# Second attention of a four-layer kernel: another buffer for beta, the first gate behind both beta halves, and another order of the statistics, the decay scan and k's turn

## The chip, the cores and the metric

The kernel runs on one core of a Trainium2 chip. A core has five engines with a queue of instructions each: TensorE (PE in the profile; PEld is its weight load, which overlaps the matmuls), VectorE (DVE), ScalarE (ACT), GpSimd (POOL) and SyncE (SP, which here only issues transfers). An engine works through its own queue in order; between engines, semaphores hold an instruction back until what it needs is there. Besides these there are 16 DMA engines.

The metric is the device time of one execution, in microseconds. The kernel before took 1192.94 us, the median of three runs.

## The reference

The model has four residual layers on x (1024 tokens of 256 channels): softmax attention, a layer of 8 experts, the second attention, and a layer of 16 experts with 4 chosen for each token. Layer norms stand in front of and behind each. The change is in the second attention alone. Its reference, cut:

```python
q, k, v = hidden_states @ Wq, hidden_states @ Wk, hidden_states @ Wv
beta = jax.nn.sigmoid(hidden_states @ Wb + bb)
gate = silu(hidden_states @ Wg)
q = silu(causal_dwconv(q, qconv_w, qconv_b))     # 4 taps along the tokens, channel by channel
k = silu(causal_dwconv(k, kconv_w, kconv_b))
q = layernorm(q.reshape(Bs, Ls, H, DK), qn_w, qn_b)   # H = 16 heads, DK = DV = 128
k = layernorm(k.reshape(Bs, Ls, H, DK), kn_w, kn_b)
...
def step(S, inp):
    q_t, k_t, v_t, b_t = inp
    S = (1.0 - b) * S + b * (v_t[..., :, None] * k_t[..., None, :])
    o_t = jnp.einsum('bhvk,bhk->bhv', S, q_t)
    return (S, o_t)
_, os = lax.scan(step, S0, (qs, ks_, vs, bs))
return (o * gate) @ Wo
```

beta is one number for each token and head. The state S of a head, a 128 x 128 matrix, decays by 1 - beta with each token and takes in v times k.

## The kernel before

All matrices are float32. The normed input lies in SBUF as hT, channels on partitions, 1024 tokens along the row. The recurrence is not run token by token: the tokens are cut into 8 chunks of 128, inside a chunk the output comes from a masked product of q and k, and between chunks the state is carried on.

`attention1` (from L1032) has these parts.

- **beta and decay, once for all heads.** `shares` makes beta for one half of the tokens: two matmuls into pb (L1066) and a Sigmoid on ACT (L1069). `decays` turns beta to tokens on partitions for the values (L1079), forms decay = 1 - beta and scans it to running products prod (L1083). With the second half done, both go to DRAM as `rows` (L1089, L1090), since each head needs its own row of them spread over all partitions. beta, decay, begin and prod borrow buffers from the two-buffer pool `two` by giving the tag of a tile that is used later; beta has the tag "y".
- **`convolved`, for k and for q of each head.** Two px instructions of PE for each half of the tokens (L1115) into a PSUM tile px, of which there are two; four taps into y (the first on ACT, L1101, the other three on DVE, L1107; in head 0 for each half by itself, otherwise for all 1024 tokens at once); a Silu on ACT (L1125). Next come eight transposes of y on PE (L1134), BN statistics on DVE (L1136), and a chain of small operations: difference d of the two half means (L1143), mean (L1144), d squared (L1145, in place), variance ve (L1146 to L1149), its power -1/2 on POOL (L1150), shift (L1151). Then ACT scales the eight blocks to sn (L1155), PE transposes them back (L1163), and ACT writes kn or qn (L1164). It is a generator with a yield between these steps: the first half's px; the second half's px with taps and Silu; transposes and statistics; sn; the turn back.
- **`values`**, for two heads at once: four pv tiles (L1185), each multiplied by beta on DVE (L1190).
- **`enter(h)`** prepares a head: it calls the generators k_, q_ and v_ in a written order, computes the output gate (`gated`: two matmuls pg, L1219, for each half of the tokens, and a Silu, L1223), has the head's rows of decay and products spread by two transfers (L1238), and scans the spread decay to dec (L1253), the decay between any two tokens of a chunk. In head 0 it also calls `shares` and `decays`, and `catch_up`, which issues the turning of hT's last tiles (L281) that the layer before has left over.
- **`attend(h)`** uses the head: qg on POOL (L1280); for each half of the chunks pk (transposes of kn, L1291), ke (L1293), the scores psc (L1301), pr (L1303), pkv (L1308) and the states (L1316, L1319); then for each half po (L1327, L1331) and og, the output times the gate (L1335). After each odd head follows the output projection of two heads, 32 matmuls (L846), added up in L858 (the first one copied, L856).

**What sets the order.** `attend(h)` is a generator too, and `enter(h + 1)` is advanced by one step at each of its yields:

```python
for _ in enter(0):
    pass
for h in range(H):
    ahead = enter(h + 1) if h + 1 < H else iter(())
    for _ in attend(h):
        next(ahead, None)
    for _ in ahead:
        pass
```

So a head's preparation lies between the pieces of the head before. The framework then reorders the instructions of each engine by its own plan, except those that are `pinned` (L210, kept in program order); what results is a fixed queue for each engine. pk, psc, pkv, po, pg, pv, pb and all transposes share one PSUM pool of four tiles (tag "b1"), so that a tile's next user waits for the reader of the one four tiles ago.

A pair of heads is: the even head (its odd partner is prepared in it), then the odd head with the output projection at its end (the next pair's even head is prepared in it).

Of the kernel before, what the change touches and what calls it, by code (L numbers as in the profile page):

```python
# [10 lines left out]
AF = mybir.ActivationFunctionType  # L11
ALU = mybir.AluOpType
# [15 lines left out]
DK = 128  # L28
# [35 lines left out]
class Net:  # L64
# [967 lines left out]
    def attention1(self):  # L1032
        nc, tc, a = self.nc, self.tc, self.a
        C = P
        NC = T // C
        with ExitStack() as ctx:
# [5 lines left out]
            idr = one.tile([P, NC, C], F32, name="idr")  # L1042
# [9 lines left out]
            two = ctx.enter_context(tc.tile_pool(name="c_two", reuse_waits="tile", bufs=2))  # L1052
            beta, decay, begin, prod = (
                two.tile([H, NC, C], F32, tag=t, name=s)
                for t, s in (("y", "beta"), ("qg", "decay"), ("sn", "begin"), ("gate", "prod"))
            )

            def flat(v):
# [36 lines left out]
            def convolved(h, hh, w, cw, cb, nw, nb, z):  # L1095

                px = ps2.tile([P, T], F32, tag="x2", name="px")
                y = two.tile([P, T], F32, tag="y", name="y")
# [13 lines left out]
                for hf in range(2):  # L1112
                    c = slice(hf * HALF, (hf + 1) * HALF)
# [25 lines left out]
                def new(name):  # L1139
                    return self.small.tile([P, NC], F32, tag=name, name=name)  # L1140

                d, mean, ve, rs, shift = (new(s) for s in ("d8", "mean8", "ve8", "rs8", "shift8"))
                nc.vector.tensor_tensor(d, st[:, :, 1], st[:, :, 4], ALU.subtract)  # L1143
                nc.vector.scalar_tensor_tensor(mean, d, -0.5, st[:, :, 1], ALU.mult, ALU.add)  # L1144
                nc.vector.scalar_tensor_tensor(d, d, 0.25, d, ALU.mult, ALU.mult)  # L1145
                nc.vector.scalar_tensor_tensor(  # L1146
                    ve, st[:, :, 2], DK * EPS, st[:, :, 5], ALU.add, ALU.add
                )
                nc.vector.scalar_tensor_tensor(ve, ve, 1.0 / DK, d, ALU.mult, ALU.add)  # L1149
                nc.gpsimd.tensor_tensor(rs, ve, self.nhalf, ALU.pow)  # L1150
                nc.vector.scalar_tensor_tensor(shift, mean, -1.0, rs, ALU.mult, ALU.mult)  # L1151
                yield
                sn = two.tile([P, NC, P], F32, tag="sn", name="sn")
# [45 lines left out]
            def enter(h):  # L1199

                g, hh = divmod(h, HG)
                if hh == 0:
                    begin_group(g)
                wq, wk, wv, wg, wo, og, vb = groups[g]
                kn = two.tile([P, T], F32, tag="kn", name="kn")
                qn = two.tile([P, T], F32, tag="qn", name="qn")
                dec = two.tile([P, NC, C], F32, tag="dec", name="dec")
                spread = two.tile([P, 2, T], F32, tag="spread", name="spread")
                gate = two.tile([P, T], F32, tag="gate", name="gate")
                heads[h] = (kn, qn, dec, spread[:, 1, :], gate)  # L1210
                k_ = convolved(h, hh, wk, C_KCW, C_KCB, C_KNW, C_KNB, kn)
                q_ = convolved(h, hh, wq, C_QCW, C_QCB, C_QNW, C_QNB, qn)
                v_ = values(g) if hh == 0 else iter(())

                def gated(hf):
                    c = slice(hf * HALF, (hf + 1) * HALF)
                    pg = ps.tile([P, HALF], F32, tag="b1", name="pg")
                    for k in range(KC):
                        nc.tensor.matmul(  # L1219
                            pg, wg[:, k, hh * DK : (hh + 1) * DK], self.hT[:, k, c],  # L1220
                            start=(k == 0), stop=(k == KC - 1),
                        )
                    nc.scalar.activation(gate[:, c], pg, AF.Silu)  # L1223

                next(k_)
                if h == 0:

                    shares(0)
                    next(q_)
                    decays(0)  # L1230
                    next(v_)
                    next(v_)
                    gated(0)
                    self.catch_up(ps, len(self.todo))
                    shares(1)
                    decays(1)
                for i in range(2):
                    nc.sync.dma_start(out=spread[:, i, :], in_=rows[i, h, :].partition_broadcast(P))  # L1238
                next(k_)
                yield  # L1240
                if h > 0:
                    next(v_, None)
                    next(v_, None)
                yield
                if h > 0:
                    next(q_)
                next(q_)
                next(k_)
                yield
                next(v_, None)  # L1250
                next(v_, None)

                nc.vector.tensor_tensor_scan(  # L1253
                    dec.rearrange("p c t -> p (c t)"), spread[:, 0, :],
                    idr.rearrange("p c t -> p (c t)"), 0.0, ALU.mult, ALU.add,
                )
                yield
                next(k_)
                next(q_)
                yield  # L1260
                for hf in range(2):
                    if (h, hf) != (0, 0):
                        gated(hf)
                yield
                next(k_)
                next(q_)
                yield
                next(q_)
                yield
# [740 lines left out]
```

## Time and profile before

| | |
|---|---|
| three runs | 1192.67, 1192.94, 1194.61 us |
| profiled execution | 1203.99 us |
| its span in the profile | 1202.3 us |
| mean granted TensorE clock | 0.983 |
| instructions | 15820 |
| second attention | about 480 to 996 us |
| PE, DVE, ACT, POOL busy in these 516 us | 482.0, 364.6, 238.1, 94.7 us |

All times that follow come from the profiled execution, which took 11 us more than the median of the runs. "First scores of head h" is the start of that head's first psc matmul; the distance between two heads' first scores is the time that one head takes:

| head | first scores, us |
|---|---|
| 0 | 533.61 |
| 1 | 562.43 |
| 2 | 597.14 |
| 4 | 658.23 |
| 6 | 718.80 |
| 7 | 743.93 |
| 8 | 779.75 |
| 14 | 962.92 |
| 15 | 983.68 |

How to read the lines that follow: a row of the timeline has start, duration, engine, line, operation, tile written and tile read with partitions x elements, and a count if several were joined (x4 px matmuls and so on). A row of the waits has the engine, what stood waiting, the engine and instruction it waited for, then the sum in us, the number of times and the longest. A row of the windows has the stretch, its length and the busy time of each engine with the number of instructions.

### The profile page before, as it was taken

Reading aid. Unit: us, or ns where it says so; the run is one execution under the profiler, and the core shown is the slowest. Engines: PE = TensorE matmul, PEld = TensorE weight load, DVE = VectorE, ACT = ScalarE, POOL = GpSimd, SP = SyncE. Lnnn points to the kernel's source line nnn. Section 1 sums busy time; section 2 is a strip of 40 time slices with the busy share of each in tenths; the row PEclk is TensorE's granted clock in tenths of the full one; section 3 lists DMA queues with packets and bytes.
Section 4 is the critical chain, followed back from the end, with each engine's and each line's share of the span. In section 5 each row is a group of like instructions: output and inputs, shape, how many; then the busy total and the mean of one; then the engine's idle time right before and its main releaser. Section 6 shows DMA issues by size and latency. Waiting matters only on the chain. (4 is left out here: it accounts for less than half of the span.)

```text
span 1202.3 us, 15820 instructions
## 1 busy us (share of the span) xinstructions
PE 1124.2 (94%) x6002; PEld 688.6 (57%) x6002; DVE 707.3 (59%) x1682; ACT 519.5 (43%) x975; POOL 222.6 (19%) x209
## 2 busy tenths in 40 slices
PE   6999999998999999789999999999999987789996
PEld 3543333332457566356767676766676776447775
DVE  5876767761534335577677777777676857233224
ACT  4266666667131111445444454544444444223331
POOL 3100000000100000111111112121212124444662
PEclk9999999999999999999999999999999998899999
DMA  6000000000005101211313131222212114154844
GB/s 207 1 1 1 1 2 1 1 1 1 1 1 194 53 1 44 68 51 36 114 43 92 65 93 64 85 72 63 77 53 86 37 64 178 55 171 123 203 45 115
DMA packets 53495, 77.01 MB, mean 64 GB/s; under 512 B 7209, under 2 KB 44408, under 8 KB 53414
## 3 DMA queue, kind: packets, MB, share of 16 engines
q1 hardware_dynamic: 46886, 69.02, 18.0%
q0 software_dynamic: 6528, 6.93, 3.1%
q8 instruction: 49, 0.80, 0.3%
q14 instruction: 32, 0.26, 0.1%
HBM read 60.93 MB, written 17.00 MB: 65 GB/s over the span
## 5 line engine op out<-in xcount | busy, mean ns | idle before, releaser
L506 DVE TENSOR_REDUCE pm<-sc 128x1 f32<-128x512 f32 x256 | 163.2, 685 | 64.5 <-PE sc L570 43.2
L570 PE MATMUL sc<-qTm,kT 32*128 32x512 f32 x512 | 151.5, 644 | 1.9 <-ACT pe L588 1.9
L599 ACT ACTIVATE pe<-sc 128x512 f32<-128x512 f32 x216 | 117.8, 595 | 67.8 <-PE sc L570 47.3
L1155 ACT ACTIVATE sn<-pt,shift,rs 128x128 f32<-128x128 f32 x256 | 93.7, 470 | 106.9 <-DVE shift L1151 106.9
L501 PE MATMUL sc<-kT,qT 32*128 32x512 f32 x512 | 136.2, 637 | 1.6 <-ACT qT L460 0.8
L1115 PE MATMUL px<-hT,w_l1a 128*128 128x512 f32 x256 | 125.0, 600 | 5.4 <-DVE y L1107 5.1
L1107 DVE SCALAR_TENSOR_TENSOR y<-px,cp,y 128x1023 f32<-128x1023 f32 (+5 forms) x102 | 123.4, 1213 | 3.9 <-ACT y L1101 3.8
L1150 POOL TENSOR_TENSOR rs<-ve,nhalf 128x8 f32<-128x8 f32 x32 | 52.4, 1637 | 304.7 <-DVE ve L1149 249.9
L831 DVE TENSOR_TENSOR mid<-sg,pu 128x512 f32<-128x512 f32 (+1 forms) x50 | 32.0, 642 | 117.3 <-PE pu L828 100.8
L830 ACT ACTIVATE sg<-pg 128x512 f32<-128x512 f32 (+1 forms) x50 | 27.7, 562 | 134.2 <-PE pg L828 116.9
L232 POOL TENSOR_TENSOR rss<-ve,nhalf 128x2 f32<-128x2 f32 x12 | 8.4, 699 | 406.2 <-DVE ve L231 401.4
L557 PE MATMUL po<-pe,va 128*32 128x256 f32 (+1 forms) x872 | 79.6, 432 | 1.3 <-ACT oT L562 0.8
L570 PEld LDWEIGHTS sc<-qTm,kT 32*128 32x128 f32 x512 | 49.6, 184 | 54.3 <-issue 38.6
L1219 PE MATMUL pg<-hT,w_l1a 128*128 128x512 f32 x128 | 62.0, 610 | 9.8 <-DVE og L1335 8.2
L1765 POOL DMA_INDIRECT sums<-ys,number x39 | 57.3, 1470 | 53.0 <-ACT ys L1760 44.8
L557 PEld LDWEIGHTS po<-pe,va 128*32 128x32 f32 x872 | 17.9, 108 | 85.3 <-issue 75.5
L1115 PEld LDWEIGHTS px<-hT,w_l1a 128*128 128x128 f32 x256 | 44.0, 195 | 32.6 <-issue 30.7
L828 PE MATMUL pg<-hT,w_l0f 128*128 128x512 f32 x128 | 61.9, 605 | 0.0
L1125 ACT ACTIVATE y<-y 128x1024 f32<-128x1024 f32 x32 | 34.2, 1068 | 63.0 <-DVE y L1107 54.5
L1185 PE MATMUL pv<-w_l1a,hT 128*128 128x256 f32 x256 | 59.9, 382 | 1.4 <-DVE state L1319 0.7
L828 PE MATMUL pu<-hT,w_l0f 128*128 128x512 f32 x128 | 60.5, 594 | 0.0
L1136 DVE BATCH_NORM_STATS2 st<-pt 128x6 f32<-128x128 f32 x256 | 55.1, 283 | 5.3 <-PE pt L1134 5.3
(277 smaller groups left out, 2051.1 us busy)
## 6 DMA issues: line engine op xcount, KB each, us to landing
spread<-rows SPq DMA_DIRECT2D x32, 512.0 KB
sw<-in_e_s SPq DMA_DIRECT2D x4, 1872.0 KB
slots<-blank SPq DMA_DIRECT2D x13, 357.0 KB
xs<-slots SPq DMA_DIRECT2D x13, 357.0 KB
w<-w SPq DMA_DIRECT2D x9, 512.0 KB
w_l0f<-in_e_wg SPq DMA_DIRECT2D x4, 512.0 KB
w_l0f<-in_e_wu SPq DMA_DIRECT2D x4, 512.0 KB
w_l0f<-in_e_wd SPq DMA_DIRECT2D x4, 512.0 KB
```

What stands on the lines that cost most here:

```text
L501: nc.tensor.matmul(sc, raw[r, tt * P : (tt + 1) * P], kT[r, g, half(kh)], start=True, stop=True,)
L506: nc.vector.tensor_reduce(pm[:, tt, 2 * pair + i, kh : kh + 1], sc, AX.X, ALU.max)
L557: nc.tensor.matmul(po[0][rows(j), c], va[:, st, g * G + j, :], pe[j // 2][:, j % 2, c], start=(st == 0), stop=(st == TT - 1 and c.stop == ...
L570: nc.tensor.matmul(sc, kT[rows(j), g, st * P : (st + 1) * P], qm[rows(j), :], start=True, stop=True,)
L599: nc.scalar.activation(pe[pair][:, i, :], sc, AF.Exp, scale=scale)
L828: nc.tensor.matmul(p, w(k), self.hT[:, k, c], start=(k == 0), stop=(k == KC - 1))
L1107: nc.vector.scalar_tensor_tensor(y[:, at:hi], px[:, at - j : hi - j], column(cw + 4 * h + 3 - j), y[:, at:hi], ALU.mult, ALU.add,)
L1115: nc.tensor.matmul(px[:, c], w[:, k, hh * DK : (hh + 1) * DK], self.hT[:, k, c], start=(k == 0), stop=(k == KC - 1),)
L1155: nc.scalar.activation(sn[:, n, :], pts[n // 4][:, n % 4, :], AF.Identity, scale=rs[:, n : n + 1], bias=shift[:, n : n + 1],)
L1185: nc.tensor.matmul(pv[:, i, :, :].rearrange("p h v -> p (h v)"), self.hT[:, k, (n + i) * P : (n + i + 1) * P], wv[:, k, :], start=(k == 0) ...
L1219: nc.tensor.matmul(pg, wg[:, k, hh * DK : (hh + 1) * DK], self.hT[:, k, c], start=(k == 0), stop=(k == KC - 1),)
L1765: sent = nc.gpsimd.indirect_dma_start(out=self.sums[e % 2][:, :], out_offset=bass.IndirectOffsetOnAxis(ap=number[:, i, :].bitcast(U32), axis=0
```

## The change

Five edits, all in `attention1`:

1. beta takes the tag "qn" instead of "y".
2. `gated` no longer issues the Silu but returns it, and the callers issue it. For head 0 the Silu of the first half, which stood in front of `shares(1)`, is issued behind `decays(1)` and is pinned. For all other gates nothing changes.
3. The statistics' small operations get another order: d squared has a tile of its own (dd), and mean is issued behind the power.
4. The scan of dec is moved into `decayed()`. For head 0 it is called where it stood. For the others it is called two steps of `enter` later, behind the gates and the transposes of q.
5. The order of the generators' steps. For h > 0, k's transposes and statistics are called between q's first and second px half, not behind the second. For all heads, k's turn back (L1163, L1164) is called right behind the gates, in the step in front of where it stood.

```diff
-                for t, s in (("y", "beta"), ("qg", "decay"), ("sn", "begin"), ("gate", "prod"))
+                for t, s in (("qn", "beta"), ("qg", "decay"), ("sn", "begin"), ("gate", "prod"))
...
-                d, mean, ve, rs, shift = (new(s) for s in ("d8", "mean8", "ve8", "rs8", "shift8"))
+                d, dd, mean, ve, rs, shift = (
+                    new(s) for s in ("d8", "dd8", "mean8", "ve8", "rs8", "shift8")
+                )
                 nc.vector.tensor_tensor(d, st[:, :, 1], st[:, :, 4], ALU.subtract)
-                nc.vector.scalar_tensor_tensor(mean, d, -0.5, st[:, :, 1], ALU.mult, ALU.add)
-                nc.vector.scalar_tensor_tensor(d, d, 0.25, d, ALU.mult, ALU.mult)
                 nc.vector.scalar_tensor_tensor(
                     ve, st[:, :, 2], DK * EPS, st[:, :, 5], ALU.add, ALU.add
                 )
-                nc.vector.scalar_tensor_tensor(ve, ve, 1.0 / DK, d, ALU.mult, ALU.add)
+                nc.vector.scalar_tensor_tensor(dd, d, 0.25, d, ALU.mult, ALU.mult)
+                nc.vector.scalar_tensor_tensor(ve, ve, 1.0 / DK, dd, ALU.mult, ALU.add)
                 nc.gpsimd.tensor_tensor(rs, ve, self.nhalf, ALU.pow)
+                nc.vector.scalar_tensor_tensor(mean, d, -0.5, st[:, :, 1], ALU.mult, ALU.add)
                 nc.vector.scalar_tensor_tensor(shift, mean, -1.0, rs, ALU.mult, ALU.mult)
...
-                    nc.scalar.activation(gate[:, c], pg, AF.Silu)
+                    return lambda: nc.scalar.activation(gate[:, c], pg, AF.Silu)
+
+                def decayed():
+
+                    nc.vector.tensor_tensor_scan(
+                        dec.rearrange("p c t -> p (c t)"), spread[:, 0, :],
+                        idr.rearrange("p c t -> p (c t)"), 0.0, ALU.mult, ALU.add,
+                    )
...
-                    gated(0)
+                    open_gate = gated(0)
                     self.catch_up(ps, len(self.todo))
                     shares(1)
                     decays(1)
+                    self.pinned(open_gate())
...
                 if h > 0:
                     next(q_)
-                next(q_)
-                next(k_)
+                    next(k_)
+                    next(q_)
+                else:
+                    next(q_)
+                    next(k_)
                 yield
                 next(v_, None)
                 next(v_, None)
-
-                nc.vector.tensor_tensor_scan(
-                    dec.rearrange("p c t -> p (c t)"), spread[:, 0, :],
-                    idr.rearrange("p c t -> p (c t)"), 0.0, ALU.mult, ALU.add,
-                )
+                if h == 0:
+                    decayed()
                 yield
                 next(k_)
                 next(q_)
                 yield
                 for hf in range(2):
                     if (h, hf) != (0, 0):
-                        gated(hf)
+                        gated(hf)()
+                next(k_)
                 yield
-                next(k_)
                 next(q_)
+                if h > 0:
+                    decayed()
                 yield
                 next(q_)
                 yield
```

In the built programs, PE and DVE have as many instructions as before, ACT has two table loads fewer, and the queues of SP and POOL have the order they had. In the queue of PE, the second half of q's px now stands behind k's transposes (L1134); in that of DVE, q's three taps stand behind the statistics of k instead of ahead of them.

## The prediction

> **What bounds the kernel now.** I read the page first, then the second attention (480 to 996 us) by windows, the waits of its engines, and the timeline engine by engine. The chain of waits on the page covers only the last 225 us, behind this stage, so it says nothing about it. From the page:
>
> ```profile
> PE 1124.2 (94%) x6002; PEld 688.6 (57%) x6002; DVE 707.3 (59%) x1682; ACT 519.5 (43%) x975; POOL 222.6 (19%) x209
> ```
>
> The stage's entry is bound by a chain through all engines. In 4 us windows (length, busy PE, PEld, DVE, ACT, POOL, granted clock, DMA):
>
> ```profile
> 496.00:500.00 4.00, 1.80 (x3) 0.41 (x4) 0.00 (x0) 3.42 (x5) 0.00 (x0) 0.79 0.00 0
> ...
> 504.00:508.00 4.00, 0.00 (x1) 0.00 (x0) 3.50 (x5) 2.52 (x4) 0.00 (x0) 1.00 0.16 25
> 508.00:512.00 4.00, 2.86 (x4) 1.34 (x5) 2.00 (x4) 1.06 (x1) 0.00 (x0) 0.57 0.91 265
> ```
>
> TensorE (PE) stands still, and behind each gap it gets a lower clock. ScalarE (ACT) shows what the first gap waits for:
>
> ```profile
> 495.29 1.28 ACT L1223 ACT_TABLE_LOAD   x1
> 496.58 0.60 ACT L1223 ACTIVATE gate<-pg 128x512 f32<-128x512 f32 x1
> 497.07 1.07 ACT L281 COPY hT<-pt 128x512 f32<-128x512 f32 x2
> 498.16 1.28 ACT L1069 ACT_TABLE_LOAD   x1
> ```
>
> From there on PE is the bound. All its waits between 590 and 960 us (us, times, longest):
>
> ```profile
> PE pg L1219 <- DVE og L1335: 7.5, 17, 1.4
> PE pt L1134 <- ACT sn L1155: 3.2, 6, 0.5
> PE psc L1301 <- ACT qn L1164: 3.0, 6, 0.7
> ```
>
> That is 13.7 us for six pairs of heads. Between the first scores of head 2 (597.14) and of head 14 (962.92) lie 365.78 us: 60.96 a pair, even head 25.13 (718.80 to 743.93), odd head 35.8. VectorE (DVE) is nearly full in the even head and has room in the odd one, under the output projection L846 (709.09 to 715.99). These rows show what is done in that room now:
>
> ```profile
> 706.54 0.67 DVE L1335 TENSOR_TENSOR og<-po,gate 128x512 f32<-128x512 f32 x1
> ...
> 707.29 1.28 DVE L1107 SCALAR_TENSOR_TENSOR y<-px,cp,y 128x1023 f32<-128x1023 f32 x1
> ...
> 708.60 1.28 DVE L1107 SCALAR_TENSOR_TENSOR y<-px,cp,y 128x1022 f32<-128x1022 f32 x1
> ...
> 709.92 1.28 DVE L1107 SCALAR_TENSOR_TENSOR y<-px,cp,y 128x1021 f32<-128x1021 f32 x1
> ...
> 711.12 0.16 DVE L1149 SCALAR_TENSOR_TENSOR ve<-ve,d 128x8 f32<-128x8 f32 x1
> ```
>
> They delay k's or q's statistics by 3.6 us, but PE has 6.9 us of L846 in the meantime and loses nothing. What matters is therefore where the order of the changed program puts these three taps.
>
> **Prices**, start to start, from the rows at 700 to 760 us. PE: psc 0.89, pkv 0.89 (three: 0.67), four transposes 0.44, one px instruction (two matmuls) 0.86, po 1.56 and 1.79, one pg tile 1.75, L846 6.9. DVE: tap 1.20, scan dec 2.20, og 0.60, eight statistics 1.65, state 0.26, a small operation 0.08 (0.2 if it needs the one before). From ve over GpSimd's (POOL's) power to shift 1.97 (725.97 to 727.94), to the first sn 0.20, the fourth sn ends 1.5 after that.
>
> **Entry (beta, gate).** Two of the four table loads go, since the Silu now stands behind both Sigmoids. One stood on the path, with the gate itself: the copies of hT end at 496.5 instead of 498.14. With a PE gap of 0.7 us instead of 2.44, I price the second pb at its first run, 1.89 (484.40), not at 3.53. Beta needs no load, and decay is ready at 500.15 instead of 503.2. From there to dec it was 8.45 us over two transfers (503.2 to 511.65): 508.6. Because beta no longer holds a y buffer, q's first taps run at 493, all second-half taps are done at 507.0 (now 518.4), the two scans end at 513.05, k's statistics follow at once (shift at 517.7, now 523.26), q's shift comes at 522.6 (now 527.59), and its gate is already through. Head 0's first scores: 527.6 instead of 533.61, **-6.0**. Bounds -4 (pb and what follows stay at the low clock, 2 us) and -8.
>
> The rows 495.29 and 496.58 give 1.29 us for a load with all that belongs to it. The Trainium skill, "ScalarE: Activation LUTs", section "What ACT_TABLE_LOAD costs", states 1283 ns and a drain, 2.66 us a switch; this trace shows no drain, and by the page the entry would gain about 1.4 us more.
>
> A PE gap of about 4 us stays (502.4 to 506.4, for px of head 1, whose buffer k's taps free). The windows above show 0.57 of the clock after the present one. The skill's "TensorE: Matmul & The Clock Gate", section "HAM oscillation", warns of idle gaps over about 3.4 us; that speaks against this part, and here the clock fell after 2.44 us too. I add nothing for it, because the scans on DVE cover PE then; uncovered it is 1.4 us (3.35 instead of 1.9 at 509.14).
>
> **Even heads (order k's statistics, then q's taps; scan later).** In the order of the changed program q's three taps leave L846. They stand behind the next head's k statistics, interleaved with the chain d, ve, dd, mean, ve. They can't be earlier: the last of q's px instructions now stands behind k's transposes. Time from the even head's psc: px visible 4.2, y 1.2, taps from 5.4, ve at 9.4 (now 7.2), shift 11.3 (now 9.1). The second pr is behind ve at 9.5, and po, which in this order waits for it, starts at 10.4. From shift, DVE works without a pause: three states 0.8, k's three next taps 3.6, two og 1.2, statistics 1.65, small ones 0.35, and then dec 2.2 between mean and ve. So ve is at 21.1, shift at 23.1 (now 19.9), and the next psc, 4.3 behind shift and sn, at **27.5** instead of 25.13. PE has done one px more (11 for 10).
>
> **Odd heads (k turned beside the gates).** The second half of k's transposes needs the PSUM buffer that the fourth sn of q frees. og ends at 23.05, as now; then chain 0.5, power 1.97, 0.2, four sn 1.5: 27.1. PE has only pg 1.75 and four transposes to do and is idle from 25.3: **a new wait of 1.85**, where L846 lay so far. L846 comes behind it, and waits in addition for the second gate, which ACT has behind those four sn. L846 6.9, q's transposes 0.87, pk 0.44: next psc at **36.0**, now 35.8. The wait of psc for qn (0.46) goes, and of the waits of pg for og only some 0.1 goes.
>
> A pair is 63.5, and I add 0.2 for more restarts (a pg tile behind a wait took 1.82 instead of 1.73): **+2.8 a pair, +16.8 for six**. Bounds per pair: -2.3 (all present waits go, none comes) and +4.5 (no overlap of the 3.6 us of taps, 1.85 less the 0.9 of px that is ahead).
>
> **Heads 0 and 1** have the same order with 13 px in head 0: 31.5 and 36.3, together 67.8 for 63.53 now (533.61 to 597.14): **+4.3**; it makes up here for the matmuls with which it reaches head 0's scores (6 px instructions of later heads instead of 9). Bounds 0 and +6.
>
> **Last two heads.** No px are left to cover. q's chain now stands behind the second og, whose po waits for the eighth sn of k (14.5): shift 19.6 behind psc instead of 14.2 (977.10 - 962.92). Two gates and two kn stand between q's sn on ACT. Head 15's psc at 25.7 instead of 20.76: **+4.9**. Bounds 0 and +6.
>
> DMAs keep their order and number; in the odd head dec waits for its spread (3.6 us behind the last state, 698.56 to 702.16), which is in the 36.0. The statistics keep their five VectorE operations; dd is only a second buffer.
>
> **Sum**: -6.0 + 4.3 + 16.8 + 4.9 = +20.0 on the profiled execution's 1203.99 (span 1202.3). The median of the runs shown, 1192.94, is 11.05 lower; I carry the difference over: **1213**.
>
> **Rivals.**
> 1. *Covered statistics* (faster). If q's taps are through before the second pr is due, the chain reaches ve first, all 13.7 us of waits go, and so do the end's losses: -6.0 - 13.7 = 1173. It decides at one place: shift of the even head at 9 us or earlier behind psc. For it: DVE is idle for 1.0 to 1.8 us there. Against it: y needs px, at 4.2. 8%.
> 2. *Only the entry counts*. Extra px in the even heads fill the waits, pairs stay at 61: -6.0 and three postponed px, 2.6, give 1189.5 (3%); with the last heads' +4.9 it is 1194.4, no change (6%). Against it: PE idle at 22.3 to 23.9 with nothing in front of it that is ready.
> 3. *Worse*. +4.5 a pair, +6 at both ends: -4 + 6 + 27 + 6 = 1228; 13%. For it: ten in-order waits a pair that each may be late.
> That the change doesn't do what it says at the entry is in the bound -4.
>
> The forecast, 1203 to 1223, has 70%. About 0.2% (2.4 us) can be told from no change. Faster: rival 1 and part of rival 2, 0.11. Same: 0.06. Slower: 0.83. The range reaches from rival 2 to near rival 3, 1190 to 1227, and leaves out rival 1 and the far end.
>
> **What would show it.** Two table loads fewer; head 0's psc 6 us earlier, at about 527.6. Pairs of 63 to 64.5 us between even psc. In each pair, PE waits of 1 to 2 us of pt L1163 for sn, twice (k's second half in the odd head, q's first in the even one), and no taps between og and ve under L846. psc of head 15 about 25.7 behind that of head 14. I am wrong if even heads take 25 us or the wait in the odd head is missing; then rivals 1 or 2 hold.

## The result and the profile after

The changed kernel took **1214.07 us** (median of four runs, 1211.57 to 1217.66) against 1193.78 us before (four runs): a ratio of **1.0171**, 95% interval 1.0157 to 1.0184. That is 20.3 us slower; the forecast was 1213.

The two profiled executions differ by less, 1212.61 against 1203.99 us. The rest lies outside the change: from head 15's first scores to the end of the span the profile of before has 1202.3 - 983.68 = 218.6 us, that of after 1210.9 - 1003.52 = 207.4. The profiles of the experiments below show that this goes with the chip: the same stretch took 218.1 to 220.0 us in the eight from the two chips on which the kernel before took 1203 us, and 208.2 to 211.2 us in the four from the chip on which it took 1193.85. The profile of before looks like the first group, that of after like the second. What differs there between the chips is not shown. So in what follows the first scores (psc) of the heads are compared, not the spans.

| first scores of head, us | before | after | difference |
|---|---|---|---|
| 0 | 533.61 | 525.95 | -7.7 |
| 2 | 597.14 | 593.78 | -3.4 |
| 14 | 962.92 | 977.50 | +14.6 |
| 15 | 983.68 | 1003.52 | +19.8 |

The stage itself begins 0.7 us later in the profile of after (its first px at 483.28 us instead of 482.59). Counted from there, head 0 gains 8.4 us and head 15 loses 19.2. Between all profiles this start differs by up to 1.7 us, so single differences of first scores below that say little.

The page of the kernel after: PE is busy for the same 1124.2 us, ACT has two instructions less.

```profile
PE 1124.2 (93%) x6002; PEld 686.2 (57%) x6002; DVE 706.4 (58%) x1682; ACT 516.6 (43%) x973; POOL 222.1 (18%) x209
```

**The entry**, kernel after, in the same 4 us windows as before (length, busy PE, PEld, DVE, ACT, POOL, clock, DMA), and ACT's rows there:

```profile
496.00:500.00 4.00, 3.27 (x9) 0.81 (x8) 0.92 (x3) 1.74 (x4) 0.00 (x0) 1.00 0.00 0
...
504.00:508.00 4.00, 1.04 (x2) 0.50 (x2) 3.98 (x7) 1.15 (x3) 0.00 (x0) 0.81 1.02 336
508.00:512.00 4.00, 4.00 (x19) 3.17 (x18) 4.00 (x4) 0.91 (x1) 0.00 (x0) 0.76 0.40 163
```

```profile
499.10 0.68 ACT L1069 ACTIVATE beta<-pb,bb 16x512 f32<-16x512 f32 x1 [1.98 <-PE pb L1066]
...
500.72 1.28 ACT L1226 ACT_TABLE_LOAD   x1
502.01 0.60 ACT L1226 ACTIVATE gate<-pg 128x512 f32<-128x512 f32 x1
```

The second Sigmoid needs no load, and the one load that is left stands behind it. The first gap of PE has gone, the second (3.72 us, forecast about 4) is still there, with a clock of 0.81 and 0.76 around it.

**The pairs**, kernel after. PE's waits between 590 and 975 us (us, times, longest):

```profile
PE pt L1165 <- ACT sn L1157: 18.0, 12, 1.6
...
PE pg L1222 <- DVE og L1348: 5.3, 12, 0.9
```

The wait of the transposes for sn, 18.0 us in twelve times, is the forecast one: twice a pair. Of the old waits, pg for og has gone from 7.5 to 5.3 us; the 3.2 us of pt L1134 for sn and the 3.0 us of psc for qn are gone. The two places in PE's timeline (even head, then the end of the odd one):

```profile
745.61 0.33 PE L1165 MATMUL pt<-ident,sn 128*128 128x128 f32 x1 [1.52 <-ACT sn L1157]
```

```profile
776.86 0.66 PE L1165 MATMUL pt<-ident,sn 128*128 128x128 f32 x4 [1.58 <-ACT sn L1157]
777.35 7.17 PE L846 MATMUL po<-w_l1a,og 128*128 128x256 f32 x32
```

The second wait stands in front of L846, whose 7 us used to cover all waiting for sn. And these are q's three taps where they are now, in the even head of DVE, ahead of the ve that they used to follow:

```profile
727.22 1.28 DVE L1107 SCALAR_TENSOR_TENSOR y<-px,cp,y 128x1023 f32<-128x1023 f32 x1
...
729.93 1.27 DVE L1107 SCALAR_TENSOR_TENSOR y<-px,cp,y 128x1021 f32<-128x1021 f32 x1
731.12 0.15 DVE L1150 SCALAR_TENSOR_TENSOR ve<-ve,dd 128x8 f32<-128x8 f32 x1
731.20 0.68 DVE L1316 TENSOR_TENSOR pr<-psc,dec 128x512 f32<-128x512 f32 x1
```

### The profile page after: what moved, and what is told of

It is laid out like the page before. It is cut to its first block, busy times and chain, and to the rows that moved or that the text cites. A ratio compares the mean times of both kernels' runs of the same rounds, so it can differ in the third digit from the quotient of the medians.

```text
span 1210.9 us, 15834 instructions
## 1 busy us (share of the span) xinstructions
PE 1124.2 (93%) x6002; PEld 686.2 (57%) x6002; DVE 706.4 (58%) x1682; ACT 516.6 (43%) x973; POOL 222.1 (18%) x209
## 5 line engine op out<-in xcount | busy, mean ns | idle before, releaser
L1115 PE MATMUL px<-hT,w_l1a 128*128 128x512 f32 x256 | 127.5, 603 | 9.5 <-DVE y L1107 3.7
L1107 DVE SCALAR_TENSOR_TENSOR y<-px,cp,y 128x1023 f32<-128x1023 f32 (+6 forms) x102 | 123.2, 1211 | 5.4 <-ACT y L1101 4.5
L1101 ACT ACTIVATE y<-px,cp 128x1024 f32<-128x1024 f32 (+1 forms) x34 | 39.6, 1166 | 122.8 <-PE px L1115 116.1
L830 ACT ACTIVATE sg<-pg 128x512 f32<-128x512 f32 (+1 forms) x50 | 27.9, 561 | 133.1 <-PE pg L828 133.1
L858 DVE TENSOR_TENSOR acc<-acc,po 128x512 f32<-128x512 f32 x38 | 26.1, 687 | 77.7 <-PE po L846 77.7
L1165 PE MATMUL pt<-ident,sn 128*128 128x128 f32 x256 | 44.7, 283 | 22.5 <-ACT sn L1157 21.2
L1165 PEld LDWEIGHTS pt<-ident,sn 128*128 128x128 f32 x256 | 31.4, 140 | 57.3 <-ACT sn L1157 41.8
```

The lines of the kernel that those rows point to most:

```text
L1107: nc.vector.scalar_tensor_tensor(y[:, at:hi], px[:, at - j : hi - j], column(cw + 4 * h + 3 - j), y[:, at:hi], ALU.mult, ALU.add,)
L1115: nc.tensor.matmul(px[:, c], w[:, k, hh * DK : (hh + 1) * DK], self.hT[:, k, c], start=(k == 0), stop=(k == KC - 1),)
L1165: nc.tensor.transpose(pt[:, i, :], sn[:, hf * 4 + i, :], self.ident)
```

## The experiments

Every experiment was timed beside the kernel before on the same chip; times of before differ between chips (1193.85 to 1203.65 us), so ratios are compared. "Pair" is the mean over the six pairs from head 2's to head 14's first scores in the experiment's profile; "last" is from head 14's to head 15's. The columns behind the ratio are from one profiled execution of each kernel.

| kernel | edits | ratio (95%) | head 0 | head 2 | pair | last | head 15 |
|---|---|---|---|---|---|---|---|
| before | - | 1 | 533.6 | 597.1 | 60.96 | 20.8 | 983.7 |
| changed | 1-5 | 1.0171 (1.0157-1.0184) | 526.0 | 593.8 | 63.95 | 26.0 | 1003.5 |
| entry | 1, 2 | 0.9965 (0.9953-0.9977) | 526.2 | 592.5 | 60.92 | 20.8 | 978.8 |
| order_only | 3, 4, 5 | 1.0208 (1.0192-1.0224) | 532.2 | 596.7 | 63.91 | 26.7 | 1006.8 |
| beta_only | 1 | 0.9969 (0.9957-0.9981) | 531.6 | 590.8 | 61.03 | 21.8 | 978.8 |
| gate_only | 2 | 0.9958 (0.9945-0.9971) | 528.0 | 591.6 | 60.96 | 20.7 | 978.1 |
| turn_only | 5, k's turn | 1.0043 (1.0029-1.0057) | 533.6 | 596.8 | 61.73 | 20.8 | 987.9 |
| no_turn | all but k's turn | 1.0155 (1.0138-1.0172) | 524.8 | 592.1 | 63.58 | 25.9 | 999.4 |
| mean_only | 3 | 0.9965 (0.9951-0.9979) | 532.6 | 592.8 | 60.55 | 21.6 | 977.8 |
| ahead_only | 5, k's statistics | 1.0140 (1.0123-1.0157) | 531.8 | 596.8 | 62.26 | 27.5 | 997.8 |
| no_ahead | all but k's statistics | 0.9988 (0.9977-0.9999) | 525.1 | 590.1 | 61.06 | 21.6 | 978.1 |
| after_twoscans | 1-5, 14 scans less | 0.9980 (0.9971-0.9989) | 524.7 | 589.4 | 60.65 | 26.7 | 980.1 |
| before_twoscans | 14 scans less | 0.9927 (0.9913-0.9941) | 533.4 | 594.1 | 60.01 | 20.7 | 974.9 |
| gate_mean | 2, 3 | 0.9913 (0.9900-0.9925) | 527.7 | 588.0 | 60.53 | 21.7 | 972.8 |

after_twoscans and before_twoscans leave out 14 of the 16 scans of dec: every head from head 2 on uses the dec of head 0 or 1, so its output is not the reference's. The theory was that of the prediction: the entry gains, q's taps in the even head and a wait ahead of L846 in the odd one lose. The rivals: entry and pairs depend on each other; one edit alone makes the loss; PE's own order, not DVE's room, sets the even head.

### Entry against order

The two halves of the change, each by itself.

```diff
# entry: edits 1 and 2; order_only: all the others
-                for t, s in (("y", "beta"), ("qg", "decay"), ("sn", "begin"), ("gate", "prod"))
+                for t, s in (("qn", "beta"), ("qg", "decay"), ("sn", "begin"), ("gate", "prod"))
...
-                    gated(0)
+                    open_gate = gated(0)
...
+                    self.pinned(open_gate())
...
```

> Only edits 1 and 2 (beta's buffer, head 0's gate behind both Sigmoids); from head 2 on the queues of PE, DVE and ACT are those of before. Theory: the entry is a term of its own. In the changed kernel head 0's first scores came at 525.95 instead of 533.61, 7.66 us earlier, with 14 px instructions ahead of them instead of 17; three of them cost 3 x 0.86 = 2.6 us later on, so the net gain is 5.1 us: about 1188.7 us (ratio 0.9957), pairs of 60.9 us, first scores of head 2 at about 592. Rival: the entry's gain is given back, because heads 0 and 1 have waits that the 7.7 us only lengthen: first scores of head 2 at about 597, time within 1 us of before. Second rival: the early entry itself is what lengthens the pairs: then pairs of 64 us and a time above 1205.

> Only edits 3, 4 and 5 (statistics' order, decay scan, order of the generators' steps); the entry is that of before, and from head 2 on the queues of PE, DVE and ACT are those of the changed kernel. Theory: all of the loss is here, and it is somewhat more than the change's: pairs of 64.1 us as in the changed kernel (+17.9 for six), last heads +5.3, heads 0 and 1 about 65.2 instead of 63.5 (14 px instead of 17 in them) +1.7: together +25, about 1218.8 us (ratio 1.021). Rival: entry and pairs are not independent terms; without the early entry the pairs find their px and taps done and run in 61 us: 1194 to 1200 us.

Measured: entry 0.9965, head 2's first scores at 592.47 (4.7 us earlier; 5.1 expected) and pairs of 60.92; order_only 1.0208, pairs of 63.91, heads 0 and 1 together 64.4 us. The halves are independent terms, as far as the profiles can tell: -4.9 and +23.1 us at head 15's first scores, sum +18.2, the change itself +19.8; counted from the stage's first px, -5.5 and +24.2, sum +18.7, the change +19.2. The ratios multiply to 1.0172. The rivals that tie the pairs to the early entry fall.

### The two parts of the entry

```diff
# beta_only
-                for t, s in (("y", "beta"), ("qg", "decay"), ("sn", "begin"), ("gate", "prod"))
+                for t, s in (("qn", "beta"), ("qg", "decay"), ("sn", "begin"), ("gate", "prod"))
# gate_only
...
-                    gated(0)
+                    open_gate = gated(0)
                     self.catch_up(ps, len(self.todo))
                     shares(1)
                     decays(1)
+                    self.pinned(open_gate())
...
```

> Only edit 1, beta in another buffer; the gate's Silu still stands between the two Sigmoids. Theory: the second Sigmoid, the transfers and the scans stay where they were (first scan at 511.65, end of both 516), but q's taps of the second half are no longer behind them (they ended at 518.4), so k's statistics start at 516: first scores of head 0 about 2.4 us earlier, or with the three px instructions more that now stand ahead of them (20 instead of 17) at the same time; the time gains about 2.4 us: 1191.4. Rival: the buffer is all of the entry's gain (the table load was covered by it): 1188.7. Second rival: it is worth nothing without the gate's move: 1193.8.

> Only edit 2, head 0's gate behind both Sigmoids; beta still holds a y buffer. Theory: a table load and the gate leave the path to the second Sigmoid (two loads fewer in all), all that stands behind it comes 3 us earlier (decay 500.2 instead of 503.2, first scan 508.6 instead of 511.65, end of q's taps 515.4 instead of 518.4), and head 0's first scores come 3 us earlier, at 530.6; the time gains 2.5 to 3 us: 1191. Rival: the clock falls as far at the same place (0.79 before) or the taps behind beta still end at 518: no gain, 1193.8. Second rival: the load is all of the entry's gain: 1188.7.

Measured: 0.9969 and 0.9958. Each alone gives about what both give together (0.9965), so they are not two terms to be added. DVE's rows of before, of gate_only and of beta_only show where the first scan of dec starts:

```profile
506.97 2.68 DVE L1107 SCALAR_TENSOR_TENSOR y<-px,cp,y 128x510 f32<-128x510 f32 x4
511.65 2.29 DVE L1253 TENSOR_TENSOR_SCAN dec<-spread,idr 128x1024 f32<-128x1024 f32 x1 [2.00 <-DMA spread<-rows]
```

```profile
499.89 1.21 DVE L1083 TENSOR_TENSOR_SCAN prod<-decay,begin 16x512 f32<-16x512 f32 x1
502.63 4.05 DVE L1107 SCALAR_TENSOR_TENSOR y<-px,cp,y 128x511 f32<-128x511 f32 x6 [1.52 <-ACT y L1101]
506.59 4.46 DVE L1254 TENSOR_TENSOR_SCAN dec<-spread,idr 128x1024 f32<-128x1024 f32 x2
```

```profile
505.19 3.47 DVE L1107 SCALAR_TENSOR_TENSOR y<-px,cp,y 128x512 f32<-128x512 f32 x5
509.98 2.29 DVE L1253 TENSOR_TENSOR_SCAN dec<-spread,idr 128x1024 f32<-128x1024 f32 x1 [1.32 <-DMA spread<-rows]
```

In gate_only prod comes so early that the scan no longer waits for its transfers: it stands right behind the taps. The new buffer on top of that brings head 0's first scores only from 527.99 to 526.24, and with two px instructions fewer ahead of them (14 instead of 16, 2 x 0.86 = 1.72): nothing is gained for PE.

That the scan starts 1.7 us earlier in beta_only cannot be put down to the buffer. The second pb, with the same wait in front of it, took 3.53 us in the profile of before (first row) and 1.89 in that of beta_only (second row), where the granted clock from 498 to 502 us was 1.00 instead of 0.58 and 0.57:

```profile
498.20 3.53 PE L1066 MATMUL pb<-hT,wb 128*16 128x512 f32 x4 [2.44 <-ACT hT L281]
```

```profile
498.74 1.89 PE L1066 MATMUL pb<-hT,wb 128*16 128x512 f32 x4 [2.44 <-ACT hT L281]
```

So beta_only does not show that path. Head 0's first scores come 45.3 us behind the stage's first px in gate_only (16 px instructions ahead of them), 48.5 in beta_only (20), 43.1 in entry (14) and 51.0 in before (17). With 0.86 us taken off for each px instruction, this is 31.6, 31.3, 31.1 and 36.4 us. Some 1.7 us of it in beta_only can be the clock's: ahead_only, with neither edit and the same full clock at pb, comes to 34.7. By the times of the runs either edit alone gains all that both gain. Why the second one adds nothing is not shown. My expectations for the single edits (2.4 and 3 us) were too low, and a sum was the wrong form.

### The two halves of the generators' order

```diff
# turn_only: k's turn beside the gates
                         gated(hf)
+                next(k_)
                 yield
-                next(k_)
                 next(q_)
```

> Only one half of edit 5: k's turn called beside the gates; q's taps stay in front of the last ve in the odd head. In the queue of PE, eight transposes of sn (k's) now stand ahead of L846 instead of behind it. Theory: the second four need the PSUM tile that q's fourth sn frees, and here q's chain has three taps in it. og ends 23.4 us behind the odd head's first scores, chain and taps 4.1, power 1.97, shift and four sn 1.7: PE may go on at 31.1; it has been idle from about 25.8, so a wait of some 5.2 us per pair ahead of L846. Odd heads 40 us instead of 35.8 (the wait for qn, 0.5, goes), even heads as before at 25.1: +4 per pair, with heads 0 and 1 seven times, +28 us, ratio 1.023, more than the whole change. Rival: the transposes that leave the other side of L846 make up for the wait, as q's half is then ready earlier: ratio 1.000 to 1.005. Second rival: the wait is only the 1.6 us that it is in the changed kernel: +0.9 per pair, ratio 1.005.

> The change without the half of edit 5 that calls k's turn beside the gates. From head 2 on, q's taps stand in the even head as in the changed kernel, but all 16 transposes of sn are behind L846 again. Theory: even heads stay at 27.7 us with their waits for sn; the wait of 1.58 us ahead of L846 goes in every odd head, and the odd heads take 34.9 us (before: 35.8 with one px more) instead of 36.4; pairs 62.6 us. With the entry's 7.7 us, heads 0 and 1 at +3.7, six pairs at +1.7 and the last heads at +4: +10 us, ratio 1.0085. Rival: the wait in the odd head is covered and only moves: odd heads 36.4, ratio 1.017 as for the whole change. Second rival: k's turn is the whole loss: pairs 61 us, ratio 0.998.

Measured: 1.0043 and 1.0155; **both expectations failed.** k's turn costs 0.4 us a pair and not 4 where it stands alone (odd heads of 36.2 instead of 35.8; the pair in the table is longer because one odd head took 38.6, see the last section), and taking it out of the change gives back 0.4 us and not 1.4 (63.95 to 63.58). The rival expectations, that the wait is made up for or only moves, come near. By time turn_only lost 4.95 us, more than seven times 0.4; a long odd head like the one in the profile may be part of it. PE's row in turn_only shows why the loss is small:

```profile
771.98 0.65 PE L1163 MATMUL pt<-ident,sn 128*128 128x128 f32 x4 [0.25 <-ACT gate L1223]
```

Here the second four transposes waited 0.25 us for a gate and not for q's fourth sn. They seem to have got the PSUM tile that the gate reads, so my "needs the buffer that the fourth sn of q frees" holds for the order of the changed kernel and not for this one. And in no_turn the 1.58 us do not come back as time: one px waits 0.77 us there, and L846 0.29. Odd heads get 0.7 us shorter (35.6), and even heads 0.35 us longer (28.0), where a new wait of pt L1134 for sn stands (4.7 us in six times):

```profile
756.99 1.10 PE L1115 MATMUL px<-hT,w_l1a 128*128 128x512 f32 x2 [0.77 <-DVE d L1145]
...
774.42 5.45 PE L846 MATMUL po<-w_l1a,og 128*128 128x256 f32 x24 [0.29 <-ACT sn L1157]
```

```diff
# ahead_only: k's statistics between q's px halves (no_ahead: this taken back from the change)
                 if h > 0:
                     next(q_)
-                next(q_)
-                next(k_)
+                    next(k_)
+                    next(q_)
+                else:
+                    next(q_)
+                    next(k_)
```

> Only the other half of edit 5: k's transposes and statistics called between q's px halves. The queues come in three forms that repeat; in two of three pairs the taps have left L846. Theory: 1.7 us for two thirds of the pairs, +7 us in six pairs, heads 0 and 1 and the last two near before: ratio 1.006. Rival: this edit is the whole loss of the even heads and more, 2.7 us in every even head and 5 us at the last: +21 us, ratio 1.018. Second rival: k's statistics come earlier by the 3.6 us of taps, all waits of psc and pt for sn go: pairs 60 us, ratio 0.995.

> The change without the half of edit 5 that puts k's statistics ahead of q's second px half; all else is in. Theory, after the runs so far: that half is the loss; what is left is the entry (4.7 us at head 2's first scores), k's turn (+0.4 a pair) and the order of the small operations (-0.4 a pair): pairs of 60.9 us, last heads +0.9: about 4 us faster than before, ratio 0.9965. Rival: the half only works together with the others, and the loss of k's turn grows without it: ratio 1.004 or more.

Measured: 1.0140 and 0.9988. With this half alone the pairs lose 1.3 us on average (1.2 expected; in the profile some 0.2 of it come from one even head with a lowered clock, see the last section), and the last heads 6.7 us, which I had left out: 27.5 instead of 20.8. So the ratio is 1.0140 and not 1.006. Without this half the rest of the change is no slower than before. This half is the loss: given the others, pairs of 61.06 become 63.95, 21.6 us at the end become 26.0, and the ratio rises from 0.9988 to 1.0171. But no_ahead gained less than the 0.9965 that I had expected, and its rival (1.004) failed too: its twelve times spread from 1189.38 to 1195.20 us, and the profiled execution, with head 15 5.6 us earlier, is one of the shorter ones (1190.05). What the longer ones lost is not shown.

```diff
# mean_only
...
-                nc.vector.scalar_tensor_tensor(mean, d, -0.5, st[:, :, 1], ALU.mult, ALU.add)
-                nc.vector.scalar_tensor_tensor(d, d, 0.25, d, ALU.mult, ALU.mult)
...
-                nc.vector.scalar_tensor_tensor(ve, ve, 1.0 / DK, d, ALU.mult, ALU.add)
+                nc.vector.scalar_tensor_tensor(dd, d, 0.25, d, ALU.mult, ALU.mult)
+                nc.vector.scalar_tensor_tensor(ve, ve, 1.0 / DK, dd, ALU.mult, ALU.add)
                 nc.gpsimd.tensor_tensor(rs, ve, self.nhalf, ALU.pow)
+                nc.vector.scalar_tensor_tensor(mean, d, -0.5, st[:, :, 1], ALU.mult, ALU.add)
```

> Only edit 3, the order of the small operations. The queues then alternate between two forms: in every other pair of heads the three taps have left the room under L846 for the next even head, which has 13 px instructions, the other has 8. Theory: what costs is the place of the taps, not which edit moved them. Taken apart, the changed kernel's +3.2 us a pair are 1.6 of waiting ahead of L846 and 1.6 to 1.8 of taps in the even head; half of the pairs have the latter: about +0.9 a pair on average, +5 us in all, ratio 1.0045. Rival: the order of the small operations takes 0.1 us off the chain ahead of the power and costs nothing else: ratio 0.999 to 1.000.

Measured: 0.9965, **against the theory**. The order of the small operations (edit 3) makes the kernel faster, by more than the rival's 0.1% as well: head 2's first scores come 4.3 us earlier (0.8 of it were there at the stage's first px) and the pairs take 60.55, although in every other pair the taps have left L846. There the even heads take 28.10 us with 13 px instructions and the next 23.22 with 8; odd heads 34.0 to 34.6 and 35.5. PE's waits in mean_only:

```profile
PE po L846 <- ACT gate L1225: 4.3, 3, 1.4
PE pt L1165 <- ACT sn L1157: 3.7, 6, 1.0
PE pg L1221 <- DVE og L1337: 2.4, 8, 0.4
PE psc L1303 <- ACT qn L1166: 1.5, 3, 0.5
```

The even head with 13 px would take 25.13 + 3 x 0.86 = 27.7 by the times of before; it takes 28.1. So taps in the even head are not dear in themselves: with three px instructions more on PE beside them they cost 0.4 us. Other even heads fit this. Those of the changed kernel have 11 px, so 26.0 by the same sum, and take 27.6, 1.6 us more. Those of ahead_only with 15 px, and nine taps where the changed kernel has six, would take 29.4, and take 29.5. Dear is an even head in which DVE has the taps and PE has too little to do. Whether edit 3 gains by its shorter chain or by the places that the px instructions get with it, no run separates.

Edit 4 (the scan) was not run by itself. In no_ahead, which has it, DVE's queue from head 2 to head 14 is that of mean_only, which does not: there the moved line moved nothing. In the built programs it left the queues as they were in the orders of before and of the changed kernel too, but no run shows this.

### Is DVE what the even head ends on?

```diff
# after_twoscans: all heads use the dec of head 0 or 1 (before_twoscans: the same on the kernel before)
...
-                dec = two.tile([P, NC, C], F32, tag="dec", name="dec")
+                if h < HG:
+                    decs[hh] = two.tile([P, NC, C], F32, tag="dec", name="dec")
+                dec = decs[hh]
...
-                if h > 0:
+                if 0 < h < HG:
                     decayed()
```

> The changed kernel, but only heads 0 and 1 scan their dec; all later heads take the dec of head 0 or 1, so that 14 scans of 2.2 us on DVE are left out (the spread transfers stay) and the output of those heads is not the reference's. The queues of PE and DVE are otherwise those of the changed kernel. Theory: with q's taps in the even head, DVE is what the even head ends on (no pause from 5.6 to 23.2 us behind its first scores but 1.2): without the scan q's shift comes 2.2 us earlier, the wait of PE for q's sn (1.52) goes, and even heads take 26.1 instead of 27.6. In the odd head og no longer stands behind the scan and its transfer; the waits for og (0.8 and 0.2) and part of the wait ahead of L846 go: about 34.2 instead of 36.4. Six pairs 3.7 us shorter each, 25 us in all against the changed kernel, ratio to before 0.996. Rival: PE's own work (the px instruction more) or the px tiles bound the even head, DVE's room does not matter: even heads 27.6, odd heads at most 1 us shorter, ratio 1.012.

> The kernel before with the same 14 scans left out (the planner then puts the px instructions of two pairs together otherwise). Theory: here DVE has room in every odd head, PE waits only 2.3 us a pair, and the scan is mostly beside PE's work: a pair gains at most 1 us (the waits for og behind the scan), ratio 0.995 to 0.999. Rival: the scans cost the same in both orders, as DVE is the bound either way: 3.7 us a pair, ratio 0.979.

This is where the scan stands in the even head of the changed kernel, in the chain to q's shift, for which the pt at 745.61 above waits:

```profile
740.73 2.29 DVE L1230 TENSOR_TENSOR_SCAN dec<-spread,idr 128x1024 f32<-128x1024 f32 x1
742.94 0.14 DVE L1150 SCALAR_TENSOR_TENSOR ve<-ve,dd 128x8 f32<-128x8 f32 x1
744.90 0.17 DVE L1153 SCALAR_TENSOR_TENSOR shift<-mean,rs 128x8 f32<-128x8 f32 x1 [1.81 <-POOL rs L1151]
```

Measured: 0.9980 (0.996 expected) and 0.9927 (0.995 to 0.999 expected). The same 14 scans are worth 22.8 us in the changed kernel (0.9980 / 1.0171 = 0.9812 of 1214) and 8.7 us in the one before; by pair 3.3 and 0.95 us. The second number is not the scans alone, as the planner gave that kernel another order (8 and 17 px in its even heads), and 3.0 of its 8.7 us are gained ahead of head 2. In the changed kernel even heads fall from 27.6 to 25.56 (26.1 expected), odd ones from 36.3 to 35.1 (34.2 expected). PE's queue is that of the changed kernel, and the wait for q's sn is gone from it:

```profile
732.14 1.02 PE L1115 MATMUL px<-hT,w_l1a 128*128 128x512 f32 x2
733.00 0.27 PE L1165 MATMUL pt<-ident,sn 128*128 128x128 f32 x1
```

The rival, PE's own work as the bound of the even head, falls: with the same work in the same order it takes 2 us less once DVE has 2.2 us less to do. In the even head the scan did not wait for its transfer, so what goes there is its time on DVE. In the odd heads waits ahead of L846 stay, the longest for a gate, 0.79:

```profile
761.01 0.66 PE L1165 MATMUL pt<-ident,sn 128*128 128x128 f32 x4 [0.79 <-ACT gate L1229]
762.06 0.66 PE L1165 MATMUL pt<-ident,sn 128*128 128x128 f32 x4 [0.39 <-ACT sn L1157]
```

### A version that beats both

Edits 2 and 3 alone:

> Edits 2 and 3 alone on the kernel before: the gate behind both Sigmoids, and the order of the small operations. Each alone gave 0.9958 and 0.9965. Theory: they act in different places (the entry; the pairs and heads 0 and 1), but both take from the idle time of heads 0 and 1, so they add up only in part: 0.993, faster than each alone and than both kernels. Rival: full sum, 0.9923. Second rival: heads 0 and 1 were all of the gain of either one: 0.996.

Measured: **0.9913** (0.9900 to 0.9925), 1184.1 us against 1193.85, and faster than the changed kernel by 2.5%. That is the rival and not my theory (0.993): the two add up in full (0.9958 x 0.9965 = 0.9923): the entry at 527.7, head 2's first scores at 588.0, pairs of 60.53.

## Why the prediction was right, step by step

- **Sum.** +20.0 us forecast, +20.3 measured, and +19.8 at head 15's first scores. That it is hit so closely is luck: the errors of the terms cancel (entry -7.7 for -6.0, six pairs +17.9 for +16.8, last heads +5.3 for +4.9). That the difference of the two profiled executions is 8.6 shows that the 11 us carried over belonged to the stretch behind this stage.
- **Entry**, 527.6 forecast, 525.95 measured: -7.7 instead of -6.0, and -8.4 counted from the stage's first px, which is beyond the bound of -8. The mis-sized term is the way from decay to dec, 8.45 us taken over from before; it took 6.85. In it were two taps and a wait of 1.3 us ahead of prod's scan and 2.0 us of waiting for the transfer; now the scan starts at 507.39, at the end of the taps, not at 508.6. k's shift came at 516.33 (517.7 forecast), q's at 521.09 (522.6). The Trainium skill's page "ScalarE: Activation LUTs", section "What ACT_TABLE_LOAD costs", gives 2.66 us with a drain; here too the next operation started 1.29 us behind the load (500.72 to 502.01), so the extra gain is not from there.
- **Entry as one term.** I had priced the gate's move and the buffer as one chain that needs both. The runs show that either edit alone has all of the gain. The low clock at the second pb, which I took from the kernel before as given, is also not always there: in beta_only pb took 1.89 us behind the same wait.
- **Heads 0 and 1**, 67.8 forecast, 67.83 measured.
- **Even heads**, 27.5 forecast, 27.6 measured, and so by the steps: behind the first scores (721.66) the taps start at 5.56 (5.4 forecast), ve at 9.46 (9.4), shift at 11.43 (11.3), po at 10.58 (10.4), the second shift at 23.24 (23.1). That DVE sets it was argued then; the changed kernel without the 14 scans shows it. My words "nearly full in the even head" do not fit the windows: before, DVE is busy for 16.3 of 25.1 us in the even head and for 27.9 of 35.8 in the odd one. What is full is a stretch, 14.5 of the 15.7 us from the first of q's taps to the ve behind the scan in the changed kernel. The scan does stand later there, as forecast, but no run shows that the line moved for it ("scan later") did that.
- **Odd heads**, 36.0 forecast, 36.3 measured, with the wait ahead of L846 at 1.58 (1.85 forecast). As a row of the trace this was right, and the price of the odd head, +0.2 forecast and +0.5 measured, was near. As a cause of the loss the wait is small: it can be taken away and 0.4 us a pair come back, because other waits fill its place.
- **Last two heads**, 25.7 forecast, 26.02 measured (shift 19.65 behind psc, 19.6 forecast). What I did not see is PE standing still for the second pr, which here too is behind the taps, with no px left beside it:

```profile
982.45 0.83 PE L1321 MATMUL pkv<-vb,ke 128*128 128x128 f32 x6
987.76 1.23 PE L1340 MATMUL po<-pr,vb 128*128 128x128 f32 x4 [4.49 <-DVE pr L1316]
```

- **Rivals.** Covered statistics asked for the even head's shift at 9 us; it came at 11.43. "Only the entry counts" is what no_ahead comes near to, 0.9988: the change would have been that rival without the half that moves k's statistics.

Still open: why edit 3 gains, why the two parts of the entry do not add up, why each form of the queues comes out of the planner, and whether the second pr ahead of the taps would save the 4.5 us at the end; it was not tried.

## What to carry to other kernels

Here work of 3.6 us cost nothing under another engine's long job, 1.6 us in a chain on which that engine waited, and 0.4 us or less where the other engine had more to do beside it. So ask of every moved step which chain it joins and what the other engine has to do meanwhile; the busy share of a whole head does not tell. Do not add up edits before running them together: two of these did not add up at all, two others in full. Do not book a wait's length as its cost: when one of 1.58 us was taken away, others within a microsecond took most of its place. Where a planner places the instructions, read the moved queue and not the moved line; one of these five edits moved nothing that a run shows, and one that looked idle was worth 4 us.

## What the runs showed of the hardware

The same pause of PE takes its clock down in one execution and leaves it in another. Ahead of the second pb PE waits 2.44 us for the copies of hT in all seven kernels without edit 2. In five of them (before, order_only, mean_only, turn_only, before_twoscans) the clock then falls to 0.50 and pb takes 2.82 to 3.53 us; in ahead_only and beta_only it stays at 1.00 and pb takes 1.89. A wait of 2.08 us in ahead_only left the clock at 1.00 at 620 us and brought it to 0.50 at 807 us. In one odd head of turn_only PE waited 1.89 us for og; windows of 1 us there (length, busy PE, PEld, DVE, ACT, POOL, clock, DMA):

```profile
891.00:892.00 1.00, 0.99 (x2) 0.49 (x3) 1.00 (x6) 0.00 (x0) 0.00 (x0) 0.87 0.00 0
892.00:893.00 1.00, 1.00 (x2) 0.33 (x1) 1.00 (x4) 0.00 (x0) 0.00 (x0) 0.50 0.00 0
```

It stayed at 0.50 until 895 us, and this odd head took 38.6 us where the others took 36.2. Some 1.1 us of that are the longer wait itself (0.78 in the odd head before it), as DVE's scan got its transfer later (a wait of 2.45 us instead of 1.34); the rest goes with the clock. The changed kernel's waits of 1.52 and 1.58 us left the clock at 1.00 in the windows around them (744 to 748, 774 to 778 us), and so did waits of 1.85 us in no_ahead; 4.49 us at the end of the changed kernel brought 0.60 on the mean of 4 us.

So here the length of one pause does not decide: 2.08 and 2.44 us went both ways. The stretches at 0.50 between 490 and 990 us last about 3.4 us or twice that in all profiles. The Trainium skill's "TensorE: Matmul & The Clock Gate", section "HAM oscillation", warns of idle gaps over about 3.4 us; the measurement decides, and pauses of little more than half that length already cost time, in some executions.
